# Two transformer layers on one core: output weights folded in layer 1's first step, last values in halves, a norm and turn on VectorE, output rows in other cycles

## The chip, the core and the metric

The kernel runs on one core of a Trainium2 chip. Its engines are TensorE (PE, matrix products, results in PSUM), VectorE (DVE), ScalarE (ACT), GpSimd (POOL) and SyncE (SP, which here only issues transfers). Each engine works through its own instructions in order; they meet through semaphores. The metric is the device time of one execution in microseconds (us), lower is better. All matrix products are in fp32; the profile has two records for each of them.

## The reference

Two layers follow each other on an input of 2 x 1024 tokens of width 256 (`reference`, cut to what is computed):

```python
xn = _layernorm(x)
x = x + attn0(xn, Wq, Wk, Wv, Wp, bp) + ffn0(xn, W_fc, W_proj)
xn = _layernorm(x)
x = x + attn1(xn, wq_a, ..., wkv_b, wo) + ffn1(xn, w1, w2, w3)
```

`attn0` is causal attention with 16 heads of 16, whose heads are cut from the rows of the projections by a plain reshape, followed by `@ Wp.T + bp`. `ffn0` has ternary weights with a scale per group of 64, a squared ReLU and an RMS norm. `attn1` is a latent attention: 16 heads of 128 + 64 (rotary) query columns against one latent of 64 columns and one rotated key of 64, shared by all heads. Its end is what this change touches:

```python
q_absorb = w[:, :NOPE, :]
out_absorb = w[:, VH:, :]
...
x = jnp.einsum('bhst,btc->bhsc', attn, kv)
x = jnp.einsum('bhsc,hdc->bhsd', x, out_absorb)
x = x.transpose(0, 2, 1, 3).reshape(b, s, NH * VH)
return x @ wo.T
```

`ffn1` has ternary weights and a sigmoid gate.

## The kernel before

Tokens lie in 16 blocks of 128. The work has two scopes, with an order written out by hand in each (`tc.manual_schedule()`): every engine gets its instructions in the order in which the Python code calls the helpers.

**Layer 0 and layer 1's projections (L194 to L1136).** It begins with the loads of x (`load_x`, L64, two transfers per batch: even blocks, odd blocks), layer norms (`ln_stats`, `ln_norm`, `ln_turn`: normalize two blocks, transpose them on PE, copy them out of PSUM on ACT), the projections, and a first group of score maxima. `ln_norm(1, 2, nc.gpsimd)` (L870) and its `ln_turn` (L879) are the first odd blocks, `ln_norm(5, 2, nc.gpsimd)` (L881) the second; POOL also updates the ternary weights in halves (`put`, L322). Then the loop over `g` (groups of four heads; 0 to 3 batch 0, 4 to 7 batch 1) and `n` (12 cycles each) mixes, in each cycle, maxima of the next group, scores and values of this one, and a piece from `fill` (feed-forward and projection work). `project_out(0, i)` (L503) turns one row block of the attention's result and returns `rest`, which multiplies it with Wp and adds it to x; seven cycles of g = 4 call it for the eight blocks of batch 0 (L1017), with `rest` one cycle later, except in cycle 5, where two blocks are done and the first `rest` follows at once. PSUM is cut into two pairs of banks for scores (`ps_pair`), three single banks (`ps_bank`) and one for values.

After the loop the eight blocks of batch 1 go through `project_out` with `down1` (layer 1's down projection of one block) and feed-forward pieces (`pump`) between them (L1045 to L1068). Then layer 1's feed-forward runs, and a list `side` is dealt among its pieces: norms, keys, queries and `fold(p)` for eight pairs of heads. `fold` multiplies weights with weights: the query side into `wm` and `w2`, and the output side, `wva` x `wo`, into `wvo` (L838 to L844). `fold_load` (L806) issues four loads per pair on SP, two pairs ahead. The first step's queries of layer 1 (`query(0)`, `query(1)`, L1114) are projected here too; their rotation is done on POOL.

**Layer 1's attention (L1147 on).** 16 steps (`steps`: batch, block pair (i, 7-i), group of eight heads), each of four cycles with two heads for each of the two blocks. In a cycle, PE computes scores of this step (`scores`), a quarter of the values of the step before (`values`, L1275), and either a projection of the next step's queries or an output product of the step before the last (`output`, L1253) with the transposes of the reciprocal sums (`inverse_T`). DVE takes the maxima from PSUM, ACT the exponentials with their sums, DVE turns the weights 32x32 (`turn_over`), POOL rotates the next queries. Scores, query projections and output products share two pairs of banks; the values have four banks of their own. The first step has no values to multiply. After the loop the last step's values are multiplied, normalized and projected (L1346 to L1360).

Of the kernel before, what the change touches and what calls it, by code (L numbers as in the profile page):

```python
# [46 lines left out]
def two_layers(ctx: ExitStack, tc: tile.TileContext, a: dict, out: bass.AP):  # L47
# [19 lines left out]

    load_x(0)

# [124 lines left out]
    with ExitStack() as scope:  # L194
# [10 lines left out]
        def ps_bank():  # L205
            return ps0.tile([P, SC], F32, tag="m", name="ps_m", bufs=3)
# [75 lines left out]

        def ln_turn(xnT, n, xn, step=1):

            pt = ps_bank()
            for k in range(2):
                for kc in range(KC):
                    nc.tensor.transpose(
                        pt[:, (2 * kc + k) * P : (2 * kc + k + 1) * P],
                        xn[:, k * E + kc * P : k * E + (kc + 1) * P], ident,  # L290
                    )
            at = n % TB
            to = xnT[n // TB].rearrange("p c (n t) -> p c n t", t=P)[:, :, at : at + step + 1 : step, :]
            nc.scalar.copy(to, pt.rearrange("p (c n t) -> p c n t", c=KC, n=2))  # L294

# [207 lines left out]
        def project_out(b, i):  # L503
            pt = ps_bank()
            for m in range(2):
                nc.tensor.transpose(
                    pt[:, m * P : (m + 1) * P], ctx_n[:, i, m * P : (m + 1) * P], ident
                )
            ctxT = l0t.tile([P, 2, P], F32, tag="ctxT", name="ctxT")
            nc.scalar.copy(ctxT.rearrange("p m t -> p (m t)"), pt[:, : 2 * P])  # L510

            def rest():
                po = ps_bank()
                for m in range(2):
                    nc.tensor.matmul(
                        po[:, :E], ctxT[:, m, :], wp[:, m, :], start=(m == 0), stop=(m == 1)
                    )
                xt = x_sb[:, b * TB + i, :]
                nc.vector.tensor_tensor(xt, xt, po[:, :E], ALU.add)

            return rest
# [284 lines left out]
        def fold_load(p):  # L806
            if p == 0:


                wm = main.tile([P, 2, NPAIR, P], F32, tag="wA", name="wm")  # L810
                folded["wm"], folded["w2"] = wm[:, 0], wm[:, 1]
                nc.sync.dma_start(folded["w2"][:R2], a["wpe2"])
                folded["wvo"] = main.tile([P, NPAIR, E], F32, tag="wB", name="wvo")
                folded["wo"] = l0.tile([P, 4, 2, E], F32, tag="ctx_n", name="fold_wo")
            t0 = l0t.tile([P, S], F32, tag="head0", name="fold0", bufs=3)
            t, at = {}, 0
            for key, width in (("wbn", LQ), ("wka", LKV), ("wva", LKV)):
                t[key] = t0[:, at : at + 2 * width].rearrange("p (h r) -> p h r", h=2)
                at += 2 * width
            t["wo"] = folded["wo"][:, p % 4]  # L820
            for key in ("wbn", "wka", "wva", "wo"):
                nc.sync.dma_start(t[key], a[key][:, 2 * p : 2 * p + 2, :])
            folded[p] = t

        def fold(p):
# [11 lines left out]
            copy_out(folded["w2"][R2:, p, :], pm[R2:, P : 2 * P])  # L837
            pv = ps_bank()  # L838
            for hh in range(2):
                nc.tensor.matmul(  # L840
                    pv[hh * LKV : (hh + 1) * LKV, :E], t["wva"][:, hh, :], t["wo"][:, hh, :],
                    start=True, stop=True,
                )
            copy_out(folded["wvo"][:, p, :], pv[:, :E])  # L844


        with tc.manual_schedule():
# [21 lines left out]
            second_w[0]()  # L869
            turns = [ln_norm(1, 2, nc.gpsimd)]  # L870
            project(0, 2, nc.vector)
            second_w[1]()
            project(1, 1)
            second_w[2]()
            second_w[3]()
            permute(0, 1)
            project(1, 0)
# [10 lines left out]

            up()
            up()  # L890

# [11 lines left out]
            def exp_table():  # L903
# [4 lines left out]
            first = {  # L908
                (-1, 0): [lambda: turn_norm(5), lambda: project(2, 1), lambda: fetch(1, 0),
                          lambda: fetch(0, 2)],  # L910
# [42 lines left out]
            deal(5, 2, 1, [lambda: ln_rstd(slice(0, TB))])  # L953

            rest = None
            for g in range(-1, NG + 1):
                this, nxt = 0 <= g < NG, g + 1 < NG
                for n in range(12 if g < NG else 2):
# [56 lines left out]
                    if 0 < g < NG and n == 2:  # L1015
                        close(g - 1, 1)
                    if g == 4 and n in (3, 4, 5, 7, 8, 9, 10):  # L1017
                        at = {3: 0, 4: 1, 5: 2, 7: 4, 8: 5, 9: 6, 10: 7}[n]
                        rest = project_out(0, at)
                        if n == 5:  # L1020
                            rest()
                            rest = project_out(0, 3)

# [17 lines left out]
            def pump():  # L1041
                if fill:
                    fill.pop(0)()

            close(NG - 1, 1)  # L1045
            side = [lambda n=n: down1(n) for n in range(TB)]
            for i in range(TB):
# [3 lines left out]
                rest = f  # L1051
                if i < 6:
                    pump()
# [38 lines left out]
            while fill:  # L1092
# [4 lines left out]
                if k == 17:  # L1097
# [24 lines left out]
                    last = [lambda c=c, n=n: queries1(1, c, n) for n in (0, 4) for c in range(2)]  # L1122
                    side += last[:2] + [lambda: query(0), last[2], lambda: query(1), last[3]]
            while side:
# [22 lines left out]
    with ExitStack() as scope:  # L1147
# [10 lines left out]
        class Step:  # L1158
            pass

        def new_step(b, i, g):
# [110 lines left out]
        with tc.manual_schedule():  # L1272
            prev, older = None, None

            def values(n0, n1):  # L1275
                for sb in range(n0, n1):
                    product(prev, sb)

            for at in range(len(steps)):
                s = new_step(*steps[at])  # L1280
                nxt = ahead(at + 1) if at + 1 < len(steps) else ()
                end = at + 1 == len(steps)
                for c in range(NCY):
# [14 lines left out]
                    if end and c == NCY - 1:  # L1298
                        for k in range(2):
                            normalize(prev, k)  # L1300
                    if narrow_last:
                        if c > 0:
# [5 lines left out]
                    else:  # L1308
                        scores(s, 1, wide)
                        turn_over(s, 0, wide[0])  # L1310
                        scores(s, 0, wide[1:])
                    k = c // 2
                    q, after = None, []
# [21 lines left out]
                    if narrow_last and not end:  # L1335
                        rest = rest[2:] + rest[:2]
                    for k_, h in rest[:-1]:
                        turn_over(s, k_, h)
                    for f in after:
                        f()  # L1340
                    turn_over(s, *rest[-1])
                    if q is not None:
                        q.rotate()
                older, prev = prev, s

            fetch_x(prev)  # L1346
            inverse(prev)
            values(prev.nsb, NSB)
            t = pair("t")
            for k in (1, 0):  # L1350
                inverse_T(prev, k, t[:, k])()
            t = pair("t")
            add = output(older, 1, t[:, 0, :E])
            normalize(prev, 1)
            add()
            values(0, prev.nsb)
            normalize(prev, 0)
            for k in (1, 0):
                t = pair("t")
                output(prev, k, t[:, 0, :E])()  # L1360

# [66 lines left out]
```

## Time and profile before

| what | us |
|---|---|
| median of three runs | 1286.08 (1285.56 to 1292.7) |
| the profiled execution | 1285.63 |
| its span, first to last instruction | 1283.6 |
| PE busy | 1253.4 |
| DVE busy | 752.6 |
| ACT busy | 640.3 |
| POOL busy | 486.6 |
| layer 1's first score matmul starts at | 687.0 |
| the last step's final score group ends at about | 1257 |

A row of the window table gives start and end of a stretch, its length, and for PE, PE's weight loads, DVE, ACT and POOL the busy time with the number of instructions, then the granted PE clock, the share of the 16 transfer engines and GB/s. A row of waits gives the waiting engine and line, who released it, the sum, how often, and the longest. A timeline row has start, length, engine, line, operation and tiles, and in brackets the idle time before it. "Busy" of PE is modelled at the ends of matmuls: each record reaches about 0.17 us over the start of the next.

### The profile page before, as it was taken

What the parts mean: (1) busy time and instruction counts of PE and PEld (TensorE: products, weight loads), DVE (VectorE), ACT (ScalarE), POOL (GpSimd) and SP (SyncE); (2) the same over time, 40 slices, a digit from 0 to 9 for tenths busy, and PEclk for the clock granted to TensorE, in tenths of its full rate; (3) what the DMA queues carried; (4) which work ended last, traced back from release to release, by engine and by line L of the source; (5) the groups of instructions that cost most, each with busy time, mean ns of one, the idle gap of its engine ahead of it and who ended that gap; (6) DMA issues with size and microseconds to landing.
All of it is one profiled execution on the core that took longest, in us unless ns stands there. A gap on an engine that the chain in (4) does not pass through costs nothing. (4 is left out here: it accounts for less than half of the span.)

```text
span 1283.6 us, 36599 instructions
## 1 busy us (share of the span) xinstructions
PE 1253.4 (98%) x15774; PEld 790.3 (62%) x15774; DVE 752.6 (59%) x1873; ACT 640.3 (50%) x1228; POOL 486.6 (38%) x512
## 2 busy tenths in 40 slices
PE   8999999999999999999998899999999999999997
PEld 6554644545546445366586567777767777777765
DVE  4966455655455555125334767766767677666773
ACT  4465456365455444433324555555555555555551
POOL 6672325344233121103126544543455335443420
PEclk9999999999999999999999999999999999999999
DMA  6421301011001000002042200000000000000000
GB/s 188 124 60 52 91 1 26 6 21 16 10 1 26 2 25 21 17 1 80 10 125 58 39 15 10 27 11 7 27 11 27 7 27 11 27 11 7 23 15 15
DMA packets 66112, 41.10 MB, mean 32 GB/s; under 512 B 37856, under 2 KB 63328, under 8 KB 65824
## 3 DMA queue, kind: packets, MB, share of 16 engines
q1 hardware_dynamic: 64960, 36.69, 11.3%
q8 instruction: 123, 2.02, 0.7%
q10 hardware_dynamic: 704, 1.05, 0.3%
q0 software_dynamic: 288, 1.05, 0.2%
q14 instruction: 37, 0.30, 0.1%
HBM read 26.18 MB, written 10.49 MB: 29 GB/s over the span
## 5 line engine op out<-in xcount | busy, mean ns | idle before, releaser
L1191 ACT ACTIVATE p<-p,nmax 128x1024 f32<-128x1024 f32 (+7 forms) x256 | 197.2, 771 | 226.7 <-DVE nmax L1187 225.9
L1180 PE MATMUL ps_s<-kT,qc 128*128 128x512 f32 (+3 forms) x768 | 279.9, 499 | 8.9 <-DVE nmax L1187 7.1
L1187 DVE CUSTOM_DVE_ANT_0 p<-ps_s,wpe 128x1024 f32<-128x1024 f32 (+7 forms) x256 | 185.6, 749 | 152.8 <-PE ps_s L1180 146.5
L461 ACT ACTIVATE p<-ps_s 128x1024 f32<-128x1024 f32 (+1 forms) x192 | 153.3, 808 | 167.6 <-PE ps_s L454 162.7
L1197 DVE STREAM_TRANSPOSE pT<-p 128x1024 f32<-128x1024 f32 (+7 forms) x256 | 191.5, 766 | 22.2 <-ACT p L1191 20.1
L1180 PEld LDWEIGHTS ps_s<-kT,qc 128*128 128x128 f32 x768 | 129.6, 191 | 108.9 <-issue 83.1
L413 PE MATMUL ps_m<-head,head 16*128 16x512 f32 (+3 forms) x672 | 177.7, 533 | 1.2 <-DVE nmx L424 0.6
L454 PE MATMUL ps_s<-head,head 17*128 17x512 f32 (+3 forms) x768 | 164.4, 533 | 0.0
L1228 PE MATMUL ps_o<-pT,vrep 32*64 32x128 f32 x9216 | 150.0, 273 | 5.9 <-issue 3.5
L178 POOL TENSOR_TENSOR qc<-t,t 32x512 f32<-32x512 f32 x120 | 152.2, 1268 | 8.1
L1228 PEld LDWEIGHTS ps_o<-pT,vrep 32*64 32x64 f32 x9216 | 133.7, 130 | 33.2 <-issue 22.7
L464 POOL TENSOR_SCALAR_AFFINE_SELECT p<-p 128x256 f32<-128x256 f32 x128 | 53.4, 421 | 224.8 <-ACT p L461 224.0
L173 POOL TENSOR_TENSOR t<-t,cosq 128x512 f32<-128x512 f32 x28 | 35.6, 1272 | 235.9 <-issue 141.2
L413 PEld LDWEIGHTS ps_m<-head,head 16*128 16x128 f32 x672 | 67.6, 183 | 85.2 <-issue 28.8
L686 PE MATMUL ps_m<-xnT,w 128*128 128x512 f32 x192 | 94.0, 617 | 0.0
L429 DVE TENSOR_REDUCE nmx<-ps_m 128x1 f32<-128x512 f32 x112 | 72.2, 686 | 32.6 <-PE ps_s L454 24.6
L424 DVE CUSTOM_DVE_ANT_0 junk<-ps_m,maskz,nmx 128x512 f32<-128x512 f32 (+3 forms) x112 | 57.6, 548 | 47.1 <-PE ps_s L454 29.7
L479 PE MATMUL ps_o<-p,v 128*32 128x512 f32 (+3 forms) x768 | 81.6, 498 | 0.0
L567 PEld LDWEIGHTS ps_m<-wpr,hT 128*128 128x128 f32 x512 | 59.9, 192 | 17.9 <-DVE nmx L429 6.8
L424 DVE CUSTOM_DVE_ANT_0 junk<-ps_m,maskz 128x512 f32<-128x512 f32 (+3 forms) x112 | 50.6, 488 | 29.7 <-PE ps_s L454 25.0
L567 PE MATMUL ps_m<-wpr,hT 128*128 128x128 f32 x512 | 66.7, 282 | 0.0
L536 PE MATMUL ps_m<-xnT,wfc 128*128 128x512 f32 x128 | 63.5, 619 | 1.4 <-ACT xnT L294 0.7
(179 smaller groups left out, 1739.4 us busy)
## 6 DMA issues: line engine op xcount, KB each, us to landing
stage<-rows SPq DMA_DIRECT2D x96, 64.0 KB, 3.1
rows<-proj SPq DMA_DIRECT2D x23, 256.0 KB, 2.5
w<-in_w SPq DMA_DIRECT2D x3, 768.0 KB, 5.1
x_sb<-in_x SPq DMA_DIRECT2D x4, 512.0 KB, 5.4
x<-x_sb SPq DMA_DIRECT2D x4, 512.0 KB, 3.2
fold_wo<-in_wo SPq DMA_DIRECT2D x8, 256.0 KB, 3.4
vrep<-kv SPq DMA_DIRECT2D x32, 64.0 KB, 2.1
xin<-x SPq DMA_DIRECT2D x16, 128.0 KB, 2.7
```

Source lines behind the costliest of these rows:

```text
L178: (even, odd)[x].tensor_tensor(self.qc[64 + 32 * x : 96 + 32 * x, hh], t1[at : at + 32], t2[at : at + 32], ALU.add,)
L413: nc.tensor.matmul(t[:, :w], quad(q, c, D0)[:, i * P : (i + 1) * P], quad(k, c, D0)[:, k0 : k0 + w], start=True, stop=True, tile_position= ...
L424: nc.vector.tensor_tensor_reduce(junk[:, :w], t[:, :w], maskz[:, SC - w :], -1.0, dst if k0 else 3.0e38, ALU.add, ALU.min, dst,)
L454: nc.tensor.matmul(t[:, c % 2, :w], quad(k, c, D0 + 1)[:, j * P : (j + 1) * P], quad(q, c, D0 + 1)[:, at : at + w], start=True, stop=True, ...
L461: nc.scalar.activation(p[:, pair[0] : pair[0] + 2, :w], t[:, :, :w], AF.Exp)
L567: nc.tensor.matmul(po[:, :P], f["h", hc // 2][:, hc % 2, t * P : (t + 1) * P], wpr[:, hc, cols], start=(hc == 0), stop=(hc == NH0 - 1),)
L686: nc.tensor.matmul(pw, w1t[f"w{i + 1}"][:, kc, hc * P : (hc + 1) * P], xnT1[n // 2][:, kc, (n % 2) * SC : (n % 2 + 1) * SC], start=(kc == ...
L1180: nc.tensor.matmul(sc[:, j * SC + n0 : j * SC + n1], s.q[k].qc[:, h // QP, h % QP, :], kT[:, s.b * S + n0 : s.b * S + n1], start=True, sto ...
L1187: nc.vector.tensor_tensor_reduce(p, sc[:, j * SC : j * SC + w], maskw[:, S - w :], -1.0, 3.0e38, ALU.add, ALU.min, nmax,)
L1191: nc.scalar.activation(p, p, AF.Exp, bias=nmax, scale=-1.0, accum_out=s.rsum[:, k, h : h + 1])
L1197: nc.vector.transpose(s.pT[:, at, h, :], s.p[k, h])
L1228: nc.tensor.matmul(s.o[64 * hh : 64 * hh + 64, c, k * P : (k + 1) * P], vrep[32 * c : 32 * c + 32, s.b * 32 + sb, :], s.pT[32 * c : 32 * c ...
```

## The change

The diff does seven things.

1. x of batch 0 is loaded in three transfers (blocks 0 and 2, blocks 4 and 6, odd blocks) in place of two.
2. The first odd norm runs on DVE instead of POOL, after the last part of the first weight updates; the second odd blocks' turn stands after the first feed-forward block instead of in cycle 0, with its copy on DVE.
3. The output rows of batch 0 go to cycles 8 to 11 of g = 3 and 3, 4, 5, 7 of g = 4, one in each.
4. At layer 0's end `project_out` of batch 1 takes a pair of score banks for its transposes, one feed-forward block stands ahead of `close` and one less behind.
5. The first step's queries move one item forward in `side`.
6. The output weights are no longer folded in layer 0. `output_weights` loads `wva` and `wo` whole, by five transfers on POOL's queue, into the buffer of turned weights that the second step will use; its eight products stand between the score groups of cycles 1 to 3 of the first step, write the values' PSUM banks, and two ACT copies take them out after the step.
7. In layer 1 the additions of steps with equally wide blocks move ahead of the last two turns; after the last step the reciprocal moves ahead of the last turn, and the remaining values are multiplied in halves of 8 and 10 blocks, with transposes and outputs between.

```diff
-    load_x(0)
+    for n in (0, 4):
+        nc.sync.dma_start(x_sb[:, n : n + 3 : 2, :], x_d[:, n : n + 3 : 2, :])
+    nc.sync.dma_start(x_sb[:, EVEN_ODD[1], :], x_d[:, EVEN_ODD[1], :])
...
-        def ln_turn(xnT, n, xn, step=1):
+        def ln_turn(xnT, n, xn, step=1, copy=nc.scalar.copy):
...
         def project_out(b, i):
-            pt = ps_bank()
+            pt = ps_bank() if b == 0 else ps_pair()[:, 0]
...
-            for key, width in (("wbn", LQ), ("wka", LKV), ("wva", LKV)):
+            for key, width in (("wbn", LQ), ("wka", LKV)):
...
-            pv = ps_bank()
-            for hh in range(2):
-                nc.tensor.matmul(
-                    pv[hh * LKV : (hh + 1) * LKV, :E], t["wva"][:, hh, :], t["wo"][:, hh, :],
-                    start=True, stop=True,
-                )
-            copy_out(folded["wvo"][:, p, :], pv[:, :E])
...
-            turns = [ln_norm(1, 2, nc.gpsimd)]
             project(0, 2, nc.vector)
             second_w[1]()
             project(1, 1)
             second_w[2]()
             second_w[3]()
+            turns = [ln_norm(1, 2)]
...
             up()
+            ln_turn(xnT, 5, turns.pop(), 2, copy=nc.vector.tensor_copy)
             up()
...
+            OUT0 = {(3, 8 + i): i for i in range(4)}
+            OUT0.update({(4, n): 4 + i for i, n in enumerate((3, 4, 5, 7))})
...
-                    side += last[:2] + [lambda: query(0), last[2], lambda: query(1), last[3]]
+                    side += [last[0], lambda: query(0), last[1], lambda: query(1)] + last[2:]
...
+        def output_weights():
+            t = att.tile([P, NSB, NH2, 32], F32, tag="pT", name="wov", bufs=2)
...
+            nc.gpsimd.dma_start(wva, a["wva"])
+            for h in range(0, NH, 4):
+                nc.gpsimd.dma_start(wo[:, h : h + 4], a["wo"][:, h : h + 4])
+            folded["wvo"] = main.tile([P, NPAIR, E], F32, tag="wB", name="wvo")
+            pv = ps.tile([P, 4, SC], F32, tag="o", name="ps_wvo").rearrange(
+                "p k (x e) -> p (k x) e", e=E
+            )
+            def product(p):
+                for hh in range(2):
+                    nc.tensor.matmul(
+                        pv[hh * LKV : (hh + 1) * LKV, p, :], wva[:, 2 * p + hh, :],
+                        wo[:, 2 * p + hh, :], start=True, stop=True,
+                    )
+            def take():
+                for k in range(0, NPAIR, 4):
+                    nc.scalar.copy(folded["wvo"][:, k : k + 4, :], pv[:, k : k + 4, :])
...
                         scores(s, 1, wide)
+                        fill()
                         turn_over(s, 0, wide[0])
                         scores(s, 0, wide[1:])
+                        if c != 2:
+                            fill()
...
+                if at == 0:
+                    fold_take()
...
             fetch_x(prev)
-            inverse(prev)
-            values(prev.nsb, NSB)
             t = pair("t")
-            for k in (1, 0):
-                inverse_T(prev, k, t[:, k])()
+            output(older, 1, t[:, 0, :E])()
             t = pair("t")
-            add = output(older, 1, t[:, 0, :E])
-            normalize(prev, 1)
-            add()
-            values(0, prev.nsb)
-            normalize(prev, 0)
-            for k in (1, 0):
-                t = pair("t")
-                output(prev, k, t[:, 0, :E])()
+            for k, n0, n1 in ((1, prev.nsb, NSB), (0, 0, prev.nsb)):
+                values(n0, (n0 + n1) // 2)
+                if k == 1:
+                    inverse_T(prev, 1, t[:, 0])()
+                else:
+                    output(prev, 1, pair("t")[:, 0, :E])()
+                values((n0 + n1) // 2, n1)
+                if k == 1:
+                    inverse_T(prev, 0, pair("t")[:, 0])()
+                normalize(prev, k)
+            output(prev, 0, pair("t")[:, 0, :E])()
```

`fill()` takes the next product from the list while the cycle is above 0; it also stands once ahead of the second score group of each cycle.

## The prediction

> **What bounds the kernel now.** I read the page first, then TensorE's own waits, then a table of windows, then the timeline of the three places where TensorE (PE) has holes.
>
> ```profile
> PE 1253.4 (98%) x15774; PEld 790.3 (62%) x15774; DVE 752.6 (59%) x1873; ACT 640.3 (50%) x1228; POOL 486.6 (38%) x512
> PE ps_s L1180 <- DVE nmax L1187: 7.1, 6, 2.9
> PE ps_o L1228 <- issue: 3.5, 3, 1.3
> PE ps_m L515 <- ACT ctxT L510: 1.2, 1, 1.2
> 560.00:600.00 40.00, 38.27 (x209) 28.81 (x208) 20.46 (x72) 13.95 (x52) 7.47 (x11) 1.00 0.16 47
> 640.00:660.00 20.00, 20.00 (x136) 13.34 (x134) 5.28 (x14) 4.12 (x12) 8.66 (x14) 1.00 0.62 188
> 687.00:724.00 37.00, 30.95 (x133) 16.92 (x133) 22.94 (x49) 18.77 (x42) 16.97 (x14) 0.91 0.44 79
> 1100.00:1258.00 158.00, 157.35 (x3148) 112.40 (x3146) 111.06 (x238) 85.28 (x188) 60.22 (x53) 1.00 0.06 18
> 1258.00:1283.60 25.60, 17.36 (x612) 14.02 (x610) 5.60 (x12) 2.55 (x6) 1.17 (x2) 1.00 0.04 13
> ```
>
> PE is busy for 98% of the span, and nearly all of its holes lie in three windows: layer 0's end (560 to 600), layer 1's first step (687 to 724, where there are no values yet to multiply; 6 us idle at a mean clock of 0.91) and the tail after 1258 (8 us idle). In 640 to 660, where the output weights are folded now, PE is full. So a matmul taken out of a full window is worth its whole time, and one put into the first step costs what the holes there do not hold.
>
> **The fold.** It removes 16 matmuls from layer 0's end, eight evacuations of 128x256 and 16 loads on SP.
>
> ```profile
> L840 PE MATMUL ps_m<-fold_wo,fold 128*64 128x256 f32 x32 | 6.9, 393 | 0.0
> 690.61 1.22 DVE L1187 CUSTOM_DVE_ANT_0 p<-ps_s,wpe 128x1024 f32<-128x1024 f32 x1 [3.74 <-POOL qc L178]
> 696.03 1.75 PE L150 MATMUL ps_t<-qnT,wm 128*128 128x128 f32 x8
> 708.17 3.43 PE L1180 MATMUL ps_s<-kT,qc 128*128 128x512 f32 x4 [2.90 <-DVE nmax L1187]
> 723.96 2.25 PE L1228 MATMUL ps_o<-pT,vrep 32*64 32x128 f32 x136 [0.19 <-DVE pT L1197]
> wfc<-in_wfc POOLq DMA_DIRECT2D x2, 512.0 KB, 6.1
> 685.37 5.21 POOL L178 TENSOR_TENSOR qc<-t 32x512 f32<-32x512 f32 x4
> 703.45 5.23 POOL L178 TENSOR_TENSOR qc<-t,t 32x512 f32<-32x512 f32 x4
> ```
>
> The trace has two records for each of these matmuls, 32 in all, 6.9 us busy and without idle before them: **-6.9 us**. DVE and ACT are idle there (5.3 and 4.1 of 20 us), so the copies saved bring nothing.
>
> **The first step.** I laid out its cycles again, with PE's first score matmul (687.02) as zero. Durations: one wide head's scores 1.7 us, the two narrow heads' 0.6, DVE's maximum of a wide head 1.15, ACT's exponential 1.15, DVE's turn 1.2, a projection 3.0 to 3.2, one fold product (four records at 0.215) 0.86. The query work of the first step moves one work item forward, past one down projection (about 1.3 us) and one transpose group (0.45): POOL's rotation ends 1.8 us earlier against PE. Before, the first maximum waited 3.74 us for POOL and began at 3.6; now at 1.85, just when PE has the scores. The second then waits for its own scores until 3.6, and PE's hole ahead of the projection shrinks. Two of the rows show PE at half clock (1.75 us for eight records that take 1.06 elsewhere; 3.43 for four that take 1.72), after its holes. With these closed I expect both gone. In my layout the maximum of cycle 1 begins at 9.9 (before 12.5), that of cycle 2 at 17.7 (19.9), of cycle 3 at 25.7 (29.4), that of step 1 at 33.4 (36.8). The eight products stand behind PE's score groups and push a narrow group by 0.4 us or less each time, already counted. At the end ACT must copy the eight products out (two copies of 128x1024, about 1.1 each) and step 1's values may not start before, since they take the same PSUM banks: 34.5 instead of 36.9. So the step gives **-2.4 us**, with the products in it. Without a cover for the copies (0.1 us is all that ACT has to spare) it would be -1.3.
>
> The products also wait for new loads: five on POOL's queue, 2.6 MB, behind the rotation that ends at 1.8. Queued behind them on POOL is step 1's rotation, ready only at about 11, so their issue (0.83 us each by the same kind of load at the start) delays nobody. The nearest row is the weight load on POOL's queue: 6.1 us to landing. The first two pieces land at 7.9 and about 8.8, and the first product stands at 9.6; later pieces are needed at 14, 18 and 26. Beside them run a 512 KB store and the 32 small vrep loads on SP; the DMA share of the step is 0.44, so there is room, and vrep itself is needed only at 34. Bounds: 0 if in time, +5 if twice the row's latency is needed. [...] But the two rows of POOL additions, 685.37 with DVE all but idle and 703.45 in the midst of its maxima and turns, differ by 0.02 us, so these DVE operations do not lock POOL out. I take 0 and keep +1.5 for the range.
>
> **The tail.** The last step's values are cut in halves with transposes and outputs between.
>
> ```profile
> 1264.59 0.94 PE L1228 MATMUL ps_o<-pT,vrep 32*64 32x128 f32 x42 [1.22 <-issue]
> 1266.85 0.66 PE L1214 MATMUL ps_t<-ident,rb 128*128 128x128 f32 x4 [0.73 <-ACT rT L1219]
> 1270.07 3.10 PE L1228 MATMUL ps_o<-pT,vrep 32*64 32x128 f32 x198 [0.84 <-DVE xT L1238]
> 1274.15 2.05 PE L1228 MATMUL ps_o<-pT,vrep 32*64 32x128 f32 x122 [0.98 <-issue]
> ```
>
> Its first row of these reads "issue": PE waited for nothing that the trace shows. Durations: an output 1.72, a transpose group 0.43, 8 blocks of values 2.06, 10 blocks 2.57, DVE's normalization 0.7. In the new order: the step before's last output to 1260.4, eight blocks to 1262.5, transposes (POOL's copies are ready at 1261.6, since the reciprocal now precedes the last turn), eight blocks to 1265.0, transposes 1265.4, ten blocks 1268.0, output 1269.7, ten blocks 1272.3, normalization 1273.2, output 1275.1, addition and store as before (3.2 after the last matmul): 1278.5 for 1283.6, -5.1. The work is the same; the holes for turns, rT and xT are what goes. Against it stand the issue holes. [...] The rows have about 1.2 us for each run of some 200 record pairs without a pause, and the new tail is denser: at two such holes -2.6, at three -1.4. I take **-2.3**, and keep 0 and -5.1.
>
> **The small moves.** Output rows of batch 0 in other cycles: the row that was multiplied at once behind its transposes is gone with its 1.2 us wait (L515 on ctxT; 1.36 with the pipeline's gap), and 0.7 and 0.3 of waits for DVE where the row and the statistics met; four rows now fall into a cycle in which DVE is half idle, for which I allow +0.5: **-1.8**. In 556 to 600 a feed-forward block now covers ACT's copy (0.7 idle at 558.84, 0.85 with the gap), and the transposes take the free score banks, which removes most of five waits of 0.17 to 0.64 for banks that ACT or DVE still read (1.7 idle, 2.6 with gaps): **-0.85 and -2.0**. The first norm on DVE and its turn: POOL saves 2.6 us ahead of the second weight update, PE's 0.6 and 0.9 us waits at 26 and 31 shift; but DVE's first maximum (30.6) waits for the second squared block on ACT, which stays where it is, and DVE is 97% busy from 35 to 55: **-0.3**, between -1.5 and +1 (the two norms and the copy lie in DVE holes of 2.2 and 5.0 us; without them +1.5). The x load in three pieces: PE's warm-up runs until 9.5, so earlier statistics gain 0.1 at most; with them 0. Additions ahead of a turn in the steps with equal blocks: two 0.4 us waits, **-0.2**.
>
> **Sum**: -6.9 -2.4 -2.3 -1.8 -0.85 -2.0 -0.3 -0.2 = -16.75. The profiled execution took 1285.63 us (span 1283.6), 0.45 under the median: 1268.9 for such a run, 1269.3 for the median.
>
> **Rivals.**
> - Loads late: the first product holds PE, and DVE behind it, because PE works in order. At twice the landing time it is +5: 1274. For: the store and vrep run beside; against: about 1 us of margin by the row.
> - The small moves and the tail give nothing (issue holes and bank waits come back elsewhere), so that only fold and first step count, -9.3: 1277. For: such holes have no visible cause. Here the change does its work but not in the places that count.
> [...]
>
> **How the numbers follow.** Forecast 0.70, on its own 1264 to 1273: the bounds of tail (-2.8, +2.3) and start (-1.2, +1.3), and half-clock spells elsewhere (the trace has two more, at 52 and 476, at most 1.7 each). Loads late 0.14; little but the fold 0.11; slower 0.05. A measurement of this kernel tells about 1% (12.9 us) from no change, so the line is 1273.2. The forecast lies under it in nine of ten cases, late loads in a third, the others not: 0.69. Slower by over 1% needs the last rival: 0.05. The rest, 0.26, is within. 1264 to 1277 leaves out the slower rival and the thin ends of the forecast.
>
> **What would show it.** No fold_wo rows and PE full in 640 to 655; the first step's row with a clock near 1.00 and no half-speed score group; products at 0.86 us with no wait for a DMA ahead of the first; values of step 1 starting about 34.5 us after the step's start, behind ACT's copies; no L515 wait of 1.2; two or three "issue" holes in a tail of about 23 us after 1258. A PE wait on the wov load, or values of step 1 later than 37, would make the prediction wrong, as would new DVE waits in the cycles that took the output rows.

## The result and the profile after

The changed kernel takes 1273.09 us (median of 4 runs, 1271.14 to 1275.24) against 1286.01 before (now also of 4 runs): ratio 0.9888, 95% interval 0.985 to 0.9926. The forecast was 1269.3, range 1264 to 1277: right in direction and inside the range, but 3.8 us too good, and just beyond the 1264 to 1273 that the main forecast had for itself. The profiled execution took 1274.54 us with a span of 1272.5, 11.1 less than before, near the slow end of its four runs.

The page's engine row, its row of instruction fetches, and PE's own waits (engine, line, releaser, sum, times, longest):

```profile
PE 1248.8 (98%) x15774; PEld 786.5 (62%) x15774; DVE 754.5 (59%) x1872; ACT 640.7 (50%) x1225; POOL 487.0 (38%) x515
...
q8 instruction: 123, 2.02, 0.7%
```

```profile
PE ps_o L1250 <- issue: 6.1, 5, 2.1
PE ps_s L1202 <- DVE nmax L1209: 2.9, 3, 1.0
...
PE ps_o L1250 <- DVE xT L1260: 1.1, 3, 0.4
...
PE ps_s L415 <- DVE nmx L426: 1.0, 1, 1.0
...
PE ps_o L1250 <- ACT wvo L1179: 0.3, 1, 0.3
```

PE still has the same 15774 matmul records and is 98% busy. The wait for VectorE's maxima fell from 7.1 to 2.9 us, the wait for ctxT (1.2) and those for `junk` are gone, and no wait for a load stands in this trace. But "issue", which was 3.5 us, is now the largest entry with 6.1.

The windows that answer to the five shown before (layer 0's end, the score folds, the first step, the late steps, the tail):

```profile
557.70:594.40 36.70, 36.52 (x203) 28.23 (x202) 20.42 (x73) 14.30 (x52) 7.45 (x11) 1.00 0.15 44
634.40:650.90 16.50, 16.50 (x107) 12.27 (x105) 4.00 (x11) 2.83 (x8) 8.72 (x14) 1.00 0.45 129
678.00:712.00 34.00, 31.86 (x158) 16.17 (x158) 23.80 (x49) 20.79 (x44) 18.63 (x19) 1.00 0.71 163
1089.10:1247.10 158.00, 157.31 (x3147) 112.22 (x3146) 111.22 (x238) 85.21 (x188) 60.27 (x52) 1.00 0.06 18
1247.10:1272.50 25.40, 17.78 (x612) 14.25 (x611) 5.59 (x12) 2.60 (x6) 1.18 (x2) 0.99 0.05 13
```

Layer 0's end is full now, the first step runs at clock 1.00 instead of 0.91, the late steps are as they were, and the tail is as long as before (25.4 against 25.6), with nearly as much idle time (7.6 against 8.2).

So that stages can be compared between traces, I took the start of the first matmul of each stage and subtracted what the half-clock spells ahead of it cost ("at full clock"). The clock record of the trace shows such a spell as 3.41 us at half speed, so each costs 1.7 where PE is busy throughout (two traces, e3 and e10, have one of twice the length); the trace before has four in its span, the one after two, and a third begins 0.4 us before its end. The untouched stages of layer 0 then agree to 0.1 us between all kernels of this study; the first row, the late steps and the tail do not, for reasons found below. "Undone" is the change of the same stage when the experiment with that part undone is compared with the changed kernel.

| stage, at full clock | forecast | before to after | undone |
|---|---|---|---|
| start to layer 0's first value matmul | -0.3 | +0.4 | -0.1 (e4) |
| layer 0 to its last value matmul (output rows) | -1.8 | -2.7 | +2.8 (e7) |
| layer 0's end | -2.85 | -3.3 | +3.4 (e6) |
| score folds to layer 1's first score matmul | -6.9 | -3.5 | +3.5 (e3) |
| first step, without its half-clock spells | +1.0 | +1.1 | -2.1 (e3), +0.6 (e5) |
| the other 15 steps to the last score matmul | -0.2 | +0.5 | |
| tail | -2.3 | -0.5 | -0.3 (e2) |
| two half-clock spells in the first step | -3.4 | -3.4 | |

(The forecast's -2.4 for the first step holds the two spells; +1.0 is what is left.) Four terms (output rows, layer 0's end, the first step and its spells) are as forecast or a little better. The 5.6 us between forecast and profile (1274.54 for 1268.9) lie in the fold (3.4), the tail (1.8), the steps and the start (0.7 each), less the 1.3 that output rows and layer 0's end gave beyond the forecast. Where a spell falls into a hole of PE it costs less than 1.7 per 3.41 us: 0.2 of the trace before and 0.6 of e3 are taken off too much, so that +1.1 is rather +0.9, and -2.1 rather -1.5. The -3.4 holds for the two profiled executions: runs of the kernel before with a mean clock of 0.998 (1281.57 us, for example) cannot have had both spells, which alone would take it to 0.997.

### The profile page after: what moved, and what is told of

Its sections match the earlier page's. It is cut to its first block, busy times and chain, and to the rows that moved or that the text cites. A ratio compares the mean times of both kernels' runs of the same rounds, so it can differ in the third digit from the quotient of the medians.

```text
span 1272.5 us, 36596 instructions
## 1 busy us (share of the span) xinstructions
PE 1248.8 (98%) x15774; PEld 786.5 (62%) x15774; DVE 754.5 (59%) x1872; ACT 640.7 (50%) x1225; POOL 487.0 (38%) x515
## 3 DMA queue, kind: packets, MB, share of 16 engines
q10 hardware_dynamic: 704, 1.05, 0.3%
## 4 chain that ended last, share of the span: by engine, by line
PE 92%; DVE 4%; ACT 2%; issue 1%; POOL 1%; DVEq 0%; ACTq 0%; POOLq 0%
PE ps_s L1202 19%; PE ps_m L415 12%; PE ps_o L1250 11%; PE ps_m L689 7%; PE ps_o L481 6%; PE ps_m L570 5%; PE ps_t L152 5%; PE ps_m L539 5%; PE ps_t L1278 4%; PE ps_m L706 3%; PE ps_m L340 3%; PE ps_t L145 2%; PE ps_m L729 1%; PE ps_s L456 1%; PE ps_m L518 1%
## 5 line engine op out<-in xcount | busy, mean ns | idle before, releaser
L175 POOL TENSOR_TENSOR t<-t,cosq 128x512 f32<-128x512 f32 x28 | 35.7, 1273 | 237.0 <-issue 141.0
L431 DVE TENSOR_REDUCE nmx<-ps_m 128x1 f32<-128x512 f32 x112 | 72.2, 685 | 32.7 <-PE ps_s L456 24.7
L426 DVE CUSTOM_DVE_ANT_0 junk<-ps_m,maskz 128x512 f32<-128x512 f32 (+3 forms) x112 | 50.5, 488 | 32.1 <-PE ps_s L456 26.3
```

## The experiments

**Where the tail's time goes.** These are the rows of the tail after the change, from the last two outputs to the last output matmul:

```profile
1249.62 2.10 PE L1250 MATMUL ps_o<-pT,vrep 32*64 32x128 f32 x128
...
1252.23 1.38 PE L1250 MATMUL ps_o<-pT,vrep 32*64 32x128 f32 x75
1254.28 1.11 PE L1250 MATMUL ps_o<-pT,vrep 32*64 32x128 f32 x53 [0.67 <-issue]
...
1256.23 1.35 PE L1250 MATMUL ps_o<-pT,vrep 32*64 32x128 f32 x71 [0.25 <-DVE xT L1260]
1258.03 1.59 PE L1250 MATMUL ps_o<-pT,vrep 32*64 32x128 f32 x89 [0.45 <-issue]
1259.55 1.99 PE L1278 MATMUL ps_t<-wvo,xT 128*128 128x256 f32 x8
1261.47 2.52 PE L1250 MATMUL ps_o<-pT,vrep 32*64 32x128 f32 x159
1266.08 0.27 PE L1250 MATMUL ps_o<-pT,vrep 32*64 32x128 f32 x1 [2.09 <-issue]
1267.20 1.99 PE L1278 MATMUL ps_t<-wvo,xT 128*128 128x256 f32 x8 [0.85 <-DVE xT L1260]
```

Count PE's matmul records from the start of the program, the first as 0: the three issue holes stand ahead of records 15381, 15509 and 15765, distances of 128 and 256. A record is a weight load and a matmul, two instructions, and the q8 row above has 123 fetches of 16 KB, one for every 256 of PE's 31548 instructions (123.2). The trace's record of q8 puts them beside the holes:

```
fetch starts (length)   first matmul behind a hole, and the time since the data landed
1251.56 (1.45)          1254.28, 1.27
1255.33 (1.17)          1258.03, 1.53
1259.08 (1.31)          (covered: an output of 2 us stands behind the crossing)
1262.89 (1.69)          1266.08, 1.50
```

Fetches follow each other 3.75 to 3.8 us apart, and each begins 0.8 to 1.05 us after PE has entered the block before. 128 records of values without a pause take only 2.1 us (first row; 16 ns each, and the last reaches further). So theory A: the holes are waits for PE's next instruction block, and dense value work is bound by one block per 3.75 us, in whatever order it stands. Theory B: the holes belong to the work around them.

e1 shifts the stream:

```diff
-            keep_warm(20)
+            keep_warm(15)
```

> The changed kernel with five of the twenty warm-up matmuls at the start left out (their result is not used), so that every later PE instruction stands 20 places, ten matmul records, earlier in PE's instruction stream. Theory A (the issue holes are waits for the next block of 256 PE instructions; a block is asked for only about when the block before it is entered, and its first instruction starts 1.3 to 1.5 us after its data landed): the four holes at records 11806, 15381, 15509 and 15765 move by exactly ten records; the one at 15765 falls behind the last output and vanishes, so the tail shortens by 1.7 to 2.3 us, and the hole at 11806 falls behind slow score matmuls and shrinks from 1.3 to under 0.4. Time about 1270. Theory B (the holes belong to the work around them, for example a wait that the trace does not show): the holes stay before the same instructions with the same length, the last of 2.1 before the last values matmul; time 1273 or, with a later clock ramp at the start, more.

Measured: 1269.11 us (1267.96 to 1270.5), ratio to before 0.9864 (0.984 to 0.9888). The same rows of e1:

```profile
1250.78 1.54 PE L1250 MATMUL ps_o<-pT,vrep 32*64 32x128 f32 x85
1253.08 0.94 PE L1250 MATMUL ps_o<-pT,vrep 32*64 32x128 f32 x43 [0.75 <-issue]
...
1254.86 1.43 PE L1250 MATMUL ps_o<-pT,vrep 32*64 32x128 f32 x81 [0.25 <-DVE xT L1260]
1256.83 1.42 PE L1250 MATMUL ps_o<-pT,vrep 32*64 32x128 f32 x79 [0.54 <-issue]
1258.18 1.99 PE L1278 MATMUL ps_t<-wvo,xT 128*128 128x256 f32 x8
1260.10 2.54 PE L1250 MATMUL ps_o<-pT,vrep 32*64 32x128 f32 x160
1263.50 1.99 PE L1278 MATMUL ps_t<-wvo,xT 128*128 128x256 f32 x8 [0.85 <-DVE xT L1260]
```

Groups of 75 + 53 and 71 + 89 became 85 + 43 and 81 + 79: the holes sit at the same places of the stream, which are ten records later in the work. The third has fallen off the end, and the tail is 2.1 us shorter. The hole ahead of record 11806 went from 1.27 to 0.64, not under 0.4 as expected: only two of the four slow score records behind that burst lie ahead of the boundary. A hole that the expectation did not list, 1.66 ahead of record 6829, is gone as well, and one of 0.30 has come ahead of 8233; with these three the other steps are 1.9 shorter. So 1.3 of the 3.5 us that e1 gains at full clock was not foreseen, though it has the same cause. Theory B is out.

e2 puts the old tail back:

```diff
+            inverse(prev)
+            values(prev.nsb, NSB)
...
-                values(n0, (n0 + n1) // 2)
```

> The changed kernel with the tail of the kernel before (values of the last step in one run, the reciprocal behind the last turn). By the prediction's sum the new tail gives 2.3 us, so the time would be 1275.4 and the part behind the start of the tail 2.3 longer. Theory A (the tail runs at the rate at which PE's instruction blocks arrive, one per 3.75 us, whatever the order of its work): the same within 0.7 us, 1273.1 plus 0 to 0.7.

Measured: 1274.12 us (1273.49 to 1274.39), 1.0 more than the changed kernel, between the two theories and inside the spread of the changed kernel's runs. The traces say more: from the last score matmul to the end, three traces with the old tail (before, e2, e10) take 27.2, 26.4 and 27.0 us, five with the new tail and a boundary ahead of its last value records (after, e3, e4, e5, e7; within three records of each other) 25.9 to 26.7, mean 26.3. That is 0.5 on the mean in place of 2.3, with ranges that touch; the one direct pair, e2 and after, has none (26.4 for 26.7). With that boundary off the last value matmul the new tail takes 24.6 (e1), 24.1 (e6), 24.3 (e8) and 24.0 (e11): the forecast gain is there, but only when the boundary falls elsewhere.

e9 measures the rate itself, by one added line ahead of the last transposes:

```diff
                 values((n0 + n1) // 2, n1)
+                values(n0, n1)
```

> The changed kernel with each of the two value sums of the last step done twice in a row in the tail (the second starts the PSUM sums anew, so they hold the same values): 512 more matmul records, four blocks of 256 PE instructions, and no other instruction. Theory A (one block per 3.75 us at most): 14 to 15.5 us longer, about 1288, with an issue hole of 1.3 to 2.1 us at every 128 records in the added stretch. Rival B (dense value matmuls run at the 2.06 us per 128 records of their rows): 8.2 us longer, 1281.3, and at most two holes more.

Measured: 1288.14 us (1285.17 to 1289.17), 15.05 more than the changed kernel. The count in the expectation was too low: the two sums have 16 and 20 blocks, so 576 records were added, 4.5 instruction blocks, not 512 and four. That the time met the expected 14 to 15.5 is therefore in part luck. By the rate of the rows (16 ns each) they would cost 9.3 us, by 3.75 us per block 16.9; at full clock the tail is 14.0 longer. The rows account for it: the issue holes of the tail sum to 7.6 us in place of 3.2, and 4.4 more with the 9.3 of matmuls makes 13.7. The end of the added stretch:

```profile
1268.42 2.52 PE L1250 MATMUL ps_o<-pT,vrep 32*64 32x128 f32 x159
1271.93 2.08 PE L1250 MATMUL ps_o<-pT,vrep 32*64 32x128 f32 x128 [0.99 <-issue]
1275.40 2.08 PE L1250 MATMUL ps_o<-pT,vrep 32*64 32x128 f32 x128 [1.39 <-issue]
1279.16 1.21 PE L1250 MATMUL ps_o<-pT,vrep 32*64 32x128 f32 x65 [1.67 <-issue]
```

Runs of exactly 128 records, each with a hole ahead, starting 3.47 and 3.76 us apart. The holes are 1.0 to 1.7 where nothing slow covers them. Rival B (8.2 us) is out, and theory A stands with a rate of about 3.5 to 3.8 us a block.

e10 is the control: the same five warm-up matmuls taken out of the kernel before.

> The kernel before, with the same five warm-up matmuls left out. Theory A: the two issue holes of its tail move by ten records inside dense value work and stay (1.2 and 1.0 us), so 0 to 1 us faster: 1284 to 1285 against 1284 to 1286. Rival H (fewer warm-up matmuls are themselves worth what the changed kernel gained by them): 3.5 to 4 us faster, 1281 to 1282.

Measured: 1282.77 us, ratio 0.9982 (0.9957 to 1.0006) to the 1284.96 of the kernel before beside it. The 2.2 us between them lie between theory A and rival H and are not clear of noise; the trace decides. The tail did not gain (27.0 for 27.2), its holes stayed, with 1.3 and 1.7 us, as theory A has it. What theory A left out are the steps, 1.4 shorter at full clock, and all of it at three crossings: compared record by record, e10 gains 1.75 at record 6827 (where the kernel before has a hole of 1.35) and 0.65 behind 10400, and loses 1.0 at 11804 (a new hole of 1.1); between them the two traces run in step to 0.02 us. So fewer warm-ups are not in themselves worth 3.5 us; where the boundaries fall is. This places the steps' +0.5 too: in the trace after, a hole of 1.27 stands ahead of record 11806, where the one before has none, and that of 1.35 is 1.66 long. The crossings cost 1.0 in sum, of which half came back at the start of the second step. Nor did the moved additions earn their -0.2: the two waits of 0.43 on ACT's rT are gone, but two of 0.42 on VectorE's xT stand in their place (in the row "DVE xT" above).

**The fold.** e3 puts the products back beside the score folds:

```diff
-            for key in ("wbn", "wka"):
+            t["wo"] = folded["wo"][:, p % 4]
+            for key in ("wbn", "wka", "wva", "wo"):
...
-            fold, fold_take = output_weights()
+            fold = []
```

> The changed kernel with the eight products of the output weights back beside the score folds of layer 0, with their loads and evacuations, and no products and copies in layer 1's first step. By the prediction's sum (0.86 us each, and at most 1.3 us for them in the first step) this costs 5 to 6.9 us: 1278 to 1280. Theory C (beside a score fold a product adds only 0.43 us, since its matmuls overlap those of the fold): layer 0's end 3.5 us longer, the first step 0.5 to 2 us shorter, so 1274.6 to 1276.

Measured: 1275.89 us (1273.1 to 1277.63), as theory C has it. At full clock layer 0 is 3.5 us longer and the first step 2.1 shorter. The timelines of PE show the 3.5, the kernel before first, then the changed kernel:

```profile
638.12 0.76 PE L832 MATMUL ps_m<-fold 128*128 128x64 f32 x5
638.62 0.43 PE L840 MATMUL ps_m<-fold_wo,fold 128*64 128x256 f32 x1
638.72 0.34 PE L832 MATMUL ps_m<-fold 128*64 128x64 f32 x3
638.89 0.60 PE L840 MATMUL ps_m<-fold_wo,fold 128*64 128x256 f32 x3
639.42 1.98 PE L686 MATMUL ps_m<-xnT,w 128*128 128x512 f32 x4
```

```profile
632.55 0.93 PE L832 MATMUL ps_m<-fold 128*128 128x64 f32 x8
633.41 1.98 PE L689 MATMUL ps_m<-xnT,w 128*128 128x512 f32 x4
```

With the product, 1.30 us pass from the fold's first record to the next projection; without it, 0.86. The product's first record starts (638.62) before the last records of the score fold (638.72), so its removal frees 0.44, not the 0.86 of its records. Why these matmuls overlap, no run shows. Sent alone in the first step of the changed kernel a product takes 0.6, from its start to the next group's:

```profile
687.83 0.65 PE L1172 MATMUL ps_wvo<-wov 128*64 128x256 f32 x4
688.41 0.71 PE L1202 MATMUL ps_s<-kT,qc 128*128 128x128 f32 x4
```

In e3 the first step also has its old hole of 2.9 again, and a half-clock spell of 6.83 us with it:

```profile
681.76:715.90 34.14, 28.81 (x118) 15.77 (x119) 21.70 (x47) 18.35 (x41) 13.44 (x12) 0.90 0.48 85
```

PE idles 5.3 of 34 us at a mean clock of 0.90; with the products it is 2.1 idle at 1.00. The first 1.2 us of the spell fall into the hole of 2.9, so that the spell cost about 2.8 and the products 1.5. Hence moving the fold nets about 3.5 - 1.5 = 2.0 at full clock, and in this pair of traces the 2.8 of the spell.

**The queries.** e5 restores their order:

```diff
-side += [last[0], lambda: query(0), last[1], lambda: query(1)] + last[2:]
+side += last[:2] + [lambda: query(0), last[2], lambda: query(1), last[3]]
```

> The changed kernel with the query work ahead of layer 1's first step in the order of the kernel before (one down projection and one transpose group later). By the prediction's layout POOL's rotation then ends 1.8 us later against PE, the first maximum starts at 3.6 instead of 2.2 us after the first score matmul, and the idle stretches that come before half-clock spells are back: first step 1.0 to 1.5 us longer at full clock, and up to two half-clock spells of 1.7 us in it, so 1274 to 1277. Rival E (the products fill the holes and set the pace, so the order is worth nothing): first maximum at 3.6, but values of step 1 at 34.0 as before, no spell, 1273.1.

Measured: 1274.93 us (1274.03 to 1277.3). The first maximum is back at 3.6 us, the first step is 0.6 longer at full clock, less than the 1.0 to 1.5 expected, and has one spell, at 683.6 to 687.0, behind holes of 1.2 and 0.4:

```profile
677.30:712.00 34.70, 32.36 (x150) 17.39 (x151) 22.14 (x48) 19.21 (x43) 18.81 (x19) 0.95 0.70 158
```

The trace before has two spells in its first step, e10, e3 and e5 one each, and the nine traces with both new parts (after, e1, e2, e4, e6, e7, e8, e9, e11) none. Each of these is one execution, and spells also fall where PE is full (see the end), so that the holes call them up is likely, not shown.

**Layer 0's end and the output rows.** e6:

```diff
-            pt = ps_bank() if b == 0 else ps_pair()[:, 0]
+            pt = ps_bank()
...
-            pump()
             close(NG - 1, 1)
...
-                if i < 5:
+                if i < 6:
```

> The changed kernel with layer 0's end of the kernel before: transposes of the last output rows in the three small PSUM banks, the feed-forward block taken behind the last close. By the prediction 2.85 us longer, with idle stretches of PE of 0.7 at the copy of oT and 0.2 to 0.6 in front of five groups back; by the traces 3.3 at full clock: about 1276. Rival F (the banks were never the limit and the gain came from elsewhere): under 1 us longer, no such waits.

The stage is 3.4 us longer, and PE's waits between 550 and 600 are the old ones:

```profile
PE ps_m L706 <- ACT junk L739: 0.7, 2, 0.4
PE ps_m L495 <- ACT oT L488: 0.7, 1, 0.7
PE ps_m L518 <- ACT junk L739: 0.6, 1, 0.6
```

Yet the median is only 1273.95 (1271.96 to 1275.95), 0.9 more. The edit moved the block boundaries two records (holes ahead of 15383 and 15511), so the last one fell behind the last value matmul, and the tail became 24.1 us long: of what the edit lost in layer 0, it got 2.6 back 700 us later. Two of its four runs also had a clock of 1.000. By its time alone this part would have been called worth next to nothing.

e7 restores `at = {3: 0, 4: 1, 5: 2, 7: 4, 8: 5, 9: 6, 10: 7}[n]` and the `rest()` of row 2.

> The changed kernel with the output rows of batch 0 in the cycles of the kernel before, one row multiplied at once behind its transposes. By the prediction 1.8 us longer (1.2 of it the wait for ctxT at that row), by the traces 2.7 at full clock: about 1275 to 1276. Rival G (VectorE's cycles that had to take the rows lose as much): the same time.

Measured: 1275.99 us (1273.45 to 1277.78), as expected, the stage 2.8 longer, with its waits back between 290 and 400:

```profile
PE ps_m L518 <- ACT ctxT L513: 1.2, 1, 1.2
PE ps_m L415 <- DVE nmx L426: 0.6, 1, 0.6
```

**The start.** e4 restores `load_x(0)`, `ln_norm(1, 2, nc.gpsimd)` and the turn in cycle 0.

> The changed kernel with the start of the kernel before: x in two loads, the first turned norms on POOL, the second turn later with its copy on ACT. By the prediction's sum the new start gives 0.3 us, so 1273.4. Theory D (from the traces: the new start gains 1.0 us by the smaller first load and loses 1.4 us or more again before 80 us, because VectorE, 97% busy there, does the norm and the copy as well): the first gain of 1.0 goes and the loss too, in sum 0.4 us faster, 1272.7, with PE's wait of 1.0 us for VectorE's maximum at 33 us gone.

Measured: 1274.01 us (1271.46 to 1274.52), no difference from the changed kernel; the median tells neither sum from the other. The trace takes the start apart. The first projection starts 1.2 later than in the trace after, but this follows the clock and not the code. PE's first warm-up matmuls are 0.21 us apart, the later ones 0.11, and the clock record is first at full at 5.8 us in the trace after, at 8.0 in the one before and at 8.5 in e4. In the nine traces with twenty warm-up matmuls this lies between 5.7 and 8.5, and the first projection starts at 10.9 to 12.2 along with it, with either start: e2, with the new one, has 7.9 and 11.9, the kernel before 8.0 and 11.9. So the 1.0 us by which the profile after is early there is the luck of one execution, and the smaller first load gains nothing that shows.

From the first projection to the first value matmul e4 takes 70.7 us, the trace after 72.1. It is 72.0 to 72.2 in all eight traces with the norm on DVE and 70.6 to 70.7 in the three with the old start. So the new start costs 1.4 us, where the prediction had a gain of 0.3; the +0.4 and -0.1 of the table hold the clock's part besides. e8 and e11, with the old norm and turn but x in three loads, take 71.4 and 71.5: half of the loss goes with the norm and the turn, half with the loads, for a reason that stays open. PE's wait for the maximum is gone in e4 as expected; waits for the turned norms (`xnT`, 1.0 and 0.7) stand in its place.

e4's trace is also 1.75 shorter in the steps, most of it at record 11806, where its hole of 1.27 is gone: again the edit moved the stream. The median does not show these gains; the four runs of e4 had clocks of 0.994 to 0.996, those of the changed kernel 0.996 to 0.998.

**A faster version.** e8 and e11 join a shift (five and eight warm-up matmuls fewer) with the old norm (x still in three loads) and move the output of the step before behind the first eight value blocks, e11 only half of it:

```diff
-            output(older, 1, t[:, 0, :E])()
...
+                    output(older, 1, pair("t")[:, 0, :E])()
                     inverse_T(prev, 1, t[:, 0])()
```

> Three edits together on the changed kernel: five warm-up matmuls fewer (PE's stream 20 instructions earlier), the norm and turn at the start back on POOL and ACT, and the output of the step before moved from the tail's start behind the first eight value blocks. If instruction blocks arrive at one per 3.75 us, a block boundary crossed 1.7 us earlier makes the rest of the tail come 1.2 to 1.7 us earlier (rival: the order of the tail does not matter, 0); the norm gives back 1.0 to 1.3 (rival, by the prediction: costs 0.3). With the 3.5 to 4.0 us of the shifted stream: 1266.0 to 1267.0; by the rivals 1269.4.

Measured: 1269.13 us (1266.49 to 1270.08), ratio 0.9874 (0.9844 to 0.9905). By the median the expectation failed: it is e1's time and that of the rivals. In the traces at full clock e8 is 1.0 us shorter than e1. The norm gave 0.7 back. The tail is 24.3 for 24.6: with the output gone from its start, the values wait 1.0 us for VectorE's last turn, which takes most of the gain. The profiled run, at clock 1.000, took 1266.49; the other three had clocks of 0.996 and 0.997.

> Eight warm-up matmuls fewer, norm and turn at the start back on POOL and ACT, and the output of the step before split: two of its four matmuls at the tail's start, where values wait 1.0 us for VectorE's last turn, two behind the first eight value blocks. Theory A: the hole near record 11806 (0.6 us with ten records) is gone, the tail 0.3 to 0.8 us shorter than with the whole output moved: 1264.0 to 1264.5 in the profile at full clock, median 1267 to 1268.5 with its half-clock spells. Rival (shift and split without effect): 1264.8 and 1269.1.

Measured: 1267.74 us (1266.34 to 1268.93), ratio 0.9864 (0.9818 to 0.991), the best median: 5.4 under the changed kernel's, with no run in common. Whether the split itself helps is not shown: at full clock the traces of e8 and e11 differ by 0.1 us. The tail is 0.3 shorter and the hole near record 11806 is gone as expected, but that ahead of record 8232, 0.25 in e8, is 1.32: a shift moves all boundaries behind it.

## Why the prediction was right, and where it was not

The direction was right, and most of the gain came where it was named: the fold, layer 0's end, the output rows and the spells of the first step. The number is 3.8 us too good because two large terms were over-estimated, for reasons that the runs show.

- **What bounds it**: right that PE does and that nothing comes from VectorE or ACT being freed. But "nearly all of its holes lie in three windows" was misread: they hold 16.0 of the 30.2 us in which PE is idle. 5.3 lie in the first 60 us, 1.9 between 300 and 400, where the output rows then gained 2.7. And "a matmul taken out of a full window is worth its whole time" failed at the fold.
- **The fold** was the largest error: "-6.9 us" should have been -3.5. "The trace has two records for each of these matmuls, 32 in all, 6.9 us busy" is true, but the busy time of a group is the union of its own records, and other records lay under it. The period of the loop with the product and without it gives the right number. The same slip helped in the first step, where I charged 0.86 for a product that takes 0.6.
- **The first step** was right to half a microsecond: the maxima of cycles 1, 2 and 3 start 10.0, 17.7 and 25.8 us after the first score matmul (forecast 9.9, 17.7, 25.7), the values at 34.0 (34.5), both spells are gone, and ACT's copies hold the values up by 0.3. The 36.9 of the sum was the second row of values before, though; the first value matmul stood at 36.3, so that the step moved by 2.3, and the layout's own 34.5 would have meant 1.8.
- **The loads** came later than I put them. "The first two pieces land at 7.9 and about 8.8": in the trace after they landed 7.0 and 9.6 us into the step, the second 0.25 before the first product (9.9). In eight of the other traces the second piece landed at 9.9 to 10.3, and the first product started 0.13 after it, at 10.0 to 10.5; so the loads did hold PE, by up to half a microsecond. In e1:

```profile
  DMA wov<-in_wo: 0.5, 1
```

That is 0.5 of the rival's 5. Some traces put this wait down to ACT, but the start follows the landing. The +1.5 that the range kept for these loads is a term that no run shows. In its place the trace after has five issues on POOL one behind the other, 0.62 us for the first and 0.53 to 0.55 for the others, while VectorE was busy for 2.36 of these 2.74 us. The second piece was issued 2.7 us into the step (1.8 and 0.83 in the layout) and took 6.9 to land, 0.8 more than the 6.1 of the row. What lengthened it, no run shows.
- **The tail**: the -5.1 of the layout and the -2.3 taken failed by the reading of the holes; the new order gave 0.5 on the mean. I took 1.2 us for a hole and two or three of them as a guess. Of the 123 block crossings in the trace after, five have an issue hole, 0.45 to 2.09 us long, all in value work (`ps_o`), where 128 records without a pause take 2.1 us. I did not count the records between the holes: 256 in the tail before (15380 to 15636), the same place in the stream after.
- **Output rows and layer 0's end** were undervalued by 0.9 and 0.45. The allowance of 0.5 for VectorE's fuller cycles was not needed; the rest stays open.
- **The start** has the opposite sign: it costs 1.4 us in place of -0.3, more than the +1 that I allowed and near the +1.5 that I kept for norms that do not fit VectorE's holes. The profile after hides 1.0 of it by an early full clock. **The moved additions** gave nothing in place of -0.2.
- **A small slip** in the tail's sum: 1275.1 and 3.2 make 1278.3, not 1278.5.
- **The rivals**: "little but the fold" (1277) had right that the holes of the tail come back, wrong that the small moves give nothing. The slower outcome, held at 0.05, did not show.

## What to carry to other kernels

Before a removed matmul is credited with its busy time, look whether its records overlap others: the period of the loop with and without it is what counts (3.5 us instead of 6.9 here). A hole marked "issue" in dense small matmuls is to be checked against the fetches, by counting instructions between holes. If it is an instruction block, rearranging the same work may gain little by itself (0.5 of 2.3 us here); ten records fewer ahead of the crossings, two of which then fell on slow matmuls or past the end, did more here (3.5 us at full clock in e1), and e9 shows what added instructions cost (15.05 us for 576 records). Since an edit can shift that grid, judge an undone edit by stages and not only by total time. And compare the clock before crediting an early start: 1 us of it was the clock's here.

## What the hardware showed unexpectedly

- PE's instruction blocks (256 instructions, 16 KB) came one per 3.5 to 3.8 us in dense value work (the tails after and in e9). No two fetches start less than 3.30 us apart in the trace before and 3.23 in the one after, though a fetch took only 0.9 to 1.9 there: ahead of the issue holes of these two, each began only 0.7 to 1.2 us after the block before it was entered, and the first matmul behind a hole started 1.3 to 1.5 after the data landed. The first 128 value records of the tail after, without a pause, took 2.1 us.
- Half-clock spells of 3.41 us, twice one of 6.83, fall at other places in each execution: none within the span of e7's trace, four in that before. Over 19 runs of the kernel before the mean clock was 0.994, over 4 of the changed kernel 0.997. The spells make most of the spread between runs: the 19 times span 10.9 us, and each multiplied by its clock lies within 1277.3 to 1280.0. What starts one outside the first step (at 35, 52, 74 to 82, 302 and 473 to 476 us, or in the last microseconds) stays open.
